# Attention in a macaron block on one core: long matrix products split over neighbouring periods, and two PSUM banks given fixed roles

## The chip, the core and the metric

The kernel runs on one core of a Trainium2 chip. The core has five engines with queues of their own: PE (TensorE, matrix products; PEld is its loading of weights), DVE (VectorE), ACT (ScalarE), POOL (GpSimd) and SP (SyncE, here the issuer of most DMAs). Each queue is worked off in its order; engines meet only through semaphores. Matrix products write to PSUM, which has eight banks of 128 partitions by 512 float32; only DVE and ACT read it here. The metric is the time of one execution in device microseconds, median over several runs; lower is better.

## The reference

The input `x` is 8 sequences of 512 tokens of 512 float32. Three steps follow each other, each on the layer-normalised `x`, and each adds to it:

```
x = x + 0.5 * ffn(layernorm(x))
x = x + attention(layernorm(x))
x = x + 0.5 * ffn(layernorm(x))
```

`ffn` is a router in which each of 16 experts chooses its 256 tokens, all with the same expert matrix: softmax of the logits, a search for the 256th largest value of each expert, and a weighted sum of one product. `attention` is differential: 16 heads of width 32 with 4 key/value heads, and every head has two score maps,

```
q, k = rope(x @ Wq), rope(x @ Wk);  v = x @ Wv
scores = softmax(causal(q_a k_a) / sqrt(D))        # a = 0, 1
diff   = softmax(causal(scores[0] - lam * scores[1]))
att    = rmsnorm(diff @ v) * rms_w * (1 - 0.8 + 0.6)
out    = att @ Wo
```

Everything is float32.

## The kernel before

The order of every engine's queue is written out by hand. `attention` walks over 176 **blocks**: for each of 8 sequences (a batch) and each of two groups of heads (`gp`, a **phase**) eleven blocks, made of the four tiles `i` of 128 queries (tile 0 is one block, tile 1 two, tiles 2 and 3 four each). The loop over `k` is a software pipeline; one turn of it is a **period**. In period `k` five blocks are in work:

- block `k + 1`: its scores on PE (`scores_next`, into banks 0 to 3);
- block `k`: `energies` on DVE (scores plus mask, and their extreme `nb`, from PSUM to `e`), `exps` on ACT (exp, with sums to `z`);
- block `k - 1`: on POOL `mask`, `factors` (after a reciprocal on DVE) and `weigh`; on DVE `difference` (`t`, `nm`);
- block `k - 2`: `exps2` on ACT, the second softmax's exp;
- block `k - 3`: `turn_pe`, transposes on PE into banks 4 and 5, and `turn_copy`, one half on DVE, one on ACT;
- block `k - 4`, if it ends a tile: `values_pe` on PE, `values_out` (`aT`) on DVE.

Beside the blocks goes work that is put into named **slots** of periods: `at(o, slot, fn)` puts it `o` periods behind the start of its phase, and `fill(k, slot)` issues it. These are, in each batch:

- `norm_steps`: layer norm of the next batch (`stats` on DVE, `apply` to `h` on POOL, `turn` to `htp` on PE, `put` to `hT` on ACT);
- `rope_steps`: ten projections, each a **long product** of four matmuls of 128x512 in one bank (L635), two readings of it on DVE (L654, L656), two DMAs that swap neighbouring partitions (L663), an add on POOL (L665);
- `value_steps`: sixteen matmuls of 128x128 for `v` (L610), read by ACT (L618);
- `finish_steps`, four times: squares on ACT, `sums` (`f_ss`, L694 and L700) on PE, `root` on ACT (L707), `turn` (`f_f`, L715) on PE, `norm` on DVE (L723), the output product `f_o` (a long product, L731) and the residual on DVE (L737).

All of these and the value products share banks 6 and 7 (`MISC`), which `misc` gives out in turn. A long product stands in slots "long" and "long 2" of one period, halves `pe(0)` and `pe(1)`, and is read in slot "mid" of the next, behind that period's energies. `PLACES` says for each of the 22 periods of a batch where the scores of the next block stand: ahead of "long" (0), between "long" and "long 2" (1), or behind both (2). Short products stand in slot "short", ahead of all that.

The last phase (`ph == 2 * B - 1`) and the periods behind it also hold the start of the second router (`early_steps`, `drain`), with MISC banks too.

Of the kernel before, what the change touches and what calls it, by code (L numbers as in the profile page):

```python
# [41 lines left out]
def macaron_kernel(  # L42
# [113 lines left out]
    LAST = ((0, 1, 1, 2, 3), (3, 4, 4, 5, 6))  # L156
# [386 lines left out]
    def attention(f0, f1, home, first_end, projections_end, drain):  # L543
        QSCALE = -1.0 / float(D) ** 0.5

        def misc(name):
            return bank(MISC, name)


        def norm_steps(at, b, st):  # L550
# [20 lines left out]
            def apply(i):  # L571
                where, tag = home["h"]
                hs[i] = where.tile([P, E], F32, name=f"h{b}_{i}", tag=tag, bufs=2)
                return nc.gpsimd.tensor_scalar(
                    hs[i], x_sb[b][:, i, :], rstd[:, i : i + 1], nmr[:, i : i + 1],
                    ALU.mult, ALU.add,
                )

            def turn(i):
                ps[i] = misc(f"htp{b}_{i}")  # L580
# [13 lines left out]
            for i in range(TPB):  # L594
                at((0, 0, 3, 3)[i], "dve", lambda i=i: stats(i))
                at((6, 6, 8, 9)[i], "pool", lambda i=i: apply(i))
                at((7, 8, 9, 10)[i], "short", lambda i=i: turn(i))
                at((7, 8, 9, 10)[i], "act mid", lambda i=i: put(i))
# [3 lines left out]
        def value_steps(at, o, b, st):  # L602
            t = {}

            def pe(h):
                if h == 0:
                    t["ps"] = misc(f"vps{b}")
# [12 lines left out]
            at(o, "long", lambda: pe(0))  # L620
            at(o, "long 2", lambda: pe(1))
            at(o + 1, "act first", act)

        def rope_steps(at, o, b, gp, n, st):
# [6 lines left out]
            def pe(h):  # L631
                if h == 0:
                    t["ps"] = misc(f"{name}_ps")
# [32 lines left out]

            at(o, "long", lambda: pe(0))
            at(o, "long 2", lambda: pe(1))
            at(o + 1, "mid", dve)
            at(o + 2, "pool", pool)  # L670

        def finish_steps(at, os, b, i, st):
# [16 lines left out]
            def sums():  # L689


                t["ss"] = misc(f"{name}_ss")
# [17 lines left out]
            def turn():  # L710

                t["f"] = misc(f"{name}_f")
# [14 lines left out]
            def pe(h):  # L727
                if h == 0:
                    t["o"] = misc(f"{name}_o")
# [172 lines left out]
        def values_pe(u):  # L902
# [3 lines left out]
            av = misc(f"av{u['id']}")  # L906
# [78 lines left out]

        def plan(ph):

            b, gp = divmod(ph, 2)
            at = placer(starts[ph])
            if gp == 0:  # L990
# [47 lines left out]
        norm_steps(pre, 0, sts[0])  # L1038
        for n in range(R + 1):
            rope_steps(pre, 12 + n, 0, 0, n, sts[0])  # L1040
# [15 lines left out]
        value_steps(placer(-2), 0, 0, sts[0])  # L1056
        for k in (-2, -1):
            for slot in order:
                fill(k, slot)

# [7 lines left out]
        for k in range(K + 13):  # L1068
            u = blocks[k] if k < K else None
            u1, uE, u2, u3 = (blocks[k - d] if 0 <= k - d < K else None for d in (1, 2, 3, 4))  # L1070
            if k in starts:
                ph = starts.index(k)
                if ph == 2 * B - 1:
# [269 lines left out]
```

## Time and profile before

| | us |
|---|---|
| median of 3 runs | 1421.61 (1421.21 to 1423.42) |
| span of the profiled execution, first to last instruction | 1420.2 |
| attention's phases, from the first scores to the last phase | 204 to 1173 |
| one batch (22 periods) in it | 129.7 |
| PE, DVE, ACT, POOL busy in the span | 1328.5, 1154.9, 1047.0, 685.4 |

The profile gives the profiled execution's own time as its span alone. It is divided by engine and by line of the kernel; a group's row gives busy time, mean duration, and the idle time of the engine ahead of it with what ended it. Matmuls are pipelined and their ends are modelled: a matmul that waits inside its row counts as busy, and durations that start before the row ahead ends overlap. Distances from start to start are therefore the better measure of what a row costs. A row of PE with x8 for four float32 matmuls is right: each is recorded as two passes. "Waits" give waiting engine and tile, releaser, sum in us, times and longest; the chain is the work that ended last, in order of time; the clock is TensorE's granted clock as a share of the full one.

### The profile page before, as it was taken

How to read it: one execution, taken by the hardware profiler on the slowest of the kernel's cores; microseconds unless marked ns; L12 is line 12 of the kernel's file. 1: busy time of each engine (PE TensorE's matmuls, PEld its weight loads, DVE VectorE, ACT ScalarE, POOL GpSimd, SP SyncE). 2: the span in 40 equal slices, each digit the busy share in tenths (PEclk: the TensorE clock that was granted, in tenths of full speed). 3: DMA queues.
4: the chain of work that ended last, by engine and by line, in shares of the span. 5: the costliest groups of instructions: out<-in, count | busy, mean ns of one | idle time of the engine just before them, and what ended most of it. 6: DMA issues, size and time to landing. Idle time of an engine off the chain costs nothing.

```text
span 1420.2 us, 30675 instructions
## 1 busy us (share of the span) xinstructions
PE 1328.5 (94%) x9774; PEld 738.4 (52%) x9774; DVE 1154.9 (81%) x4405; ACT 1047.0 (74%) x3644; POOL 685.4 (48%) x1314
## 2 busy tenths in 40 slices
PE   6999899899999999999999999999999997998998
PEld 4544444455555555555555555555455555555443
DVE  6554769899989988998999899889989989654566
ACT  3411128999899898989898998989899989844110
POOL 5433626554555455454545555554545555443230
PEclk9999988999999999999999999999999997999999
DMA  9300011000000101000000001010000001000006
GB/s 344 91 1 0 0 38 38 9 31 24 16 24 17 39 1 38 9 31 9 32 24 16 28 13 39 2 38 16 24 13 27 28 13 40 1 5 1 1 1 236
DMA packets 27554, 48.19 MB, mean 34 GB/s; under 512 B 4720, under 2 KB 6016, under 8 KB 27392
## 3 DMA queue, kind: packets, MB, share of 16 engines
q1 hardware_dynamic: 25152, 42.03, 8.3%
q10 hardware_dynamic: 2208, 4.19, 0.8%
q8 instruction: 77, 1.26, 0.4%
q14 instruction: 85, 0.70, 0.2%
q0 software_dynamic: 32, 0.01, 0.0%
HBM read 16.86 MB, written 8.39 MB: 18 GB/s over the span
## 4 chain that ended last, share of the span: by engine, by line
PE 60%; ACT 13%; DVE 10%; issue 2%; POOL 0%; ACTq 0%; DVEq 0%
PE r_ps L635 18%; PE sc L761 8%; PE f_o L731 8%; ACT e L790 7%; PE tp L882 6%; PE yps L381 6%; PE av L913 4%; DVE e L777 4%; DVE t L848 3%; ACT t L862 2%; PE vps L610 2%; PE kps L403 2%; PE f_f L715 1%; ACT eT L900 1%; PE tp L325 1%
## 5 line engine op out<-in xcount | busy, mean ns | idle before, releaser
L790 ACT ACTIVATE e<-e,nb 128x192 f32<-128x192 f32 (+7 forms) x1024 | 535.5, 532 | 6.5 <-DVE nb L777 4.3
L777 DVE CUSTOM_DVE_ANT_0 e<-sc,mpos 128x192 f32<-128x192 f32 (+7 forms) x1024 | 400.8, 453 | 23.7 <-PE sc L761 16.5
L814 POOL TENSOR_SCALAR e<-e,z 128x512 f32<-128x512 f32 (+7 forms) x512 | 295.9, 590 | 16.7
L862 ACT ACTIVATE t<-t,nm 128x512 f32<-128x512 f32 (+7 forms) x512 | 270.0, 534 | 42.2 <-DVE nm L848 42.0
L761 PE MATMUL sc<-r,r 32*128 32x64 f32 (+7 forms) x2048 | 245.3, 456 | 10.8 <-DVE nb L777 4.9
L848 DVE CUSTOM_DVE_ANT_0 t<-e,z 128x512 f32<-128x512 f32 (+7 forms) x512 | 240.6, 518 | 5.1 <-POOL e L814 4.2
L635 PE MATMUL r_ps<-hT,wq_sb 128*128 128x512 f32 x512 | 235.6, 601 | 0.1
L381 PE MATMUL yps<-we,y 128*128 128x512 f32 x456 | 216.5, 612 | 1.0 <-ACT y L388 0.7
L882 PEld LDWEIGHTS tp<-ident,t 128*128 128x128 f32 x1280 | 146.5, 144 | 135.6 <-ACT eT L900 43.3
L882 PE MATMUL tp<-ident,t 128*128 128x128 f32 x1280 | 188.6, 283 | 28.1 <-ACT eT L900 26.6
L790 ACT ACTIVATION_READ_ACCUMULATOR e<-e,nb 128x1 f32 x1024 | 202.1, 197 | 0.0
L665 POOL TENSOR_TENSOR r<-r,r_sw 128x512 f32<-128x512 f32 x80 | 103.0, 1296 | 175.8 <-DVE z L799 84.2
L761 PEld LDWEIGHTS sc<-r,r 32*128 32x128 f32 x2048 | 117.4, 188 | 90.7 <-DVE nb L777 44.6
L391 POOL TENSOR_TENSOR y<-y,eb 128x512 f32<-128x512 f32 x57 | 73.1, 1283 | 164.4 <-ACT y L388 134.3
L635 PEld LDWEIGHTS r_ps<-hT,wq_sb 128*128 128x128 f32 x512 | 93.0, 190 | 113.9 <-issue 99.6
L388 ACT COPY y<-yps 128x512 f32<-128x512 f32 x57 | 33.4, 586 | 155.6 <-PE yps L381 155.6
L828 POOL TENSOR_SCALAR_AFFINE_SELECT e<-e 128x128 f32<-128x128 f32 x256 | 79.2, 316 | 99.4 <-ACT e L790 99.4
L898 DVE COPY eT<-tp 128x512 f32<-128x512 f32 (+1 forms) x176 | 112.0, 636 | 16.6 <-PE tp L882 16.6
L381 PEld LDWEIGHTS yps<-we,y 128*128 128x128 f32 x456 | 81.3, 192 | 78.4 <-issue 73.6
L731 PE MATMUL f_o<-wo_sb,f_an 128*128 128x512 f32 x256 | 118.6, 605 | 0.0
L804 POOL TENSOR_TENSOR z<-z,over 128x4 f32<-128x4 f32 (+1 forms) x192 | 38.0, 201 | 142.6 <-DVE z L799 142.5
L862 ACT ACTIVATION_READ_ACCUMULATOR t<-t,nm 128x1 f32 x512 | 100.4, 196 | 0.0
(123 smaller groups left out, 1668.6 us busy)
## 6 DMA issues: line engine op xcount, KB each, us to landing
r_sw<-r_by SPq DMA_DIRECT2D x160, 128.0 KB, 2.0
x<-in_x_dram SPq DMA_DIRECT2D x6, 1024.0 KB, 13.2
out_dram<-x SPq DMA_DIRECT2D x6, 512.0 KB, 3.2
out_dram<-x ACTq DMA_DIRECT2D x6, 512.0 KB, 3.2
x<-in_x_dram SPq DMA_DIRECT2D x8, 256.0 KB, 8.2
we<-in_expert_w_dram SPq DMA_DIRECT2D x2, 1024.0 KB, 7.7
wq_sb<-in_wq_dram SPq DMA_DIRECT2D x1, 2048.0 KB, 13.9
wo_sb<-in_wo_dram SPq DMA_DIRECT2D x8, 128.0 KB, 2.8
```

The lines of the kernel that those rows point to most:

```text
L381: nc.tensor.matmul(held["yps"], buf[b][:, i, c * P : (c + 1) * P], held["we"][:, c, :], start=(c == 0), stop=(c == EC - 1),)
L635: nc.tensor.matmul(t["ps"], w[:, c, c0 : c0 + P], st["hT"][:, c, :], start=(c == 0), stop=(c == EC - 1),)
L665: return nc.gpsimd.tensor_add(t["out"], t["out"], t["sw"])
L731: nc.tensor.matmul(t["o"], t["an"][:, c, :], wo_sb[:, c // 2, c % 2, :], start=(c == 0), stop=(c == 3),)
L761: nc.tensor.matmul(u["sc"][j][:, part.cols], q[j * D : (j + 1) * D, q0 : q0 + P], kq["k"][j * D : (j + 1) * D, : part.n], start=True, stop ...
L777: nc.vector.tensor_tensor_reduce(out=u["e"][:, j, part.cols], in0=u["sc"][j][:, part.cols], in1=mpos[:, S - part.n :], scale=1.0, scalar=3 ...
L790: nc.scalar.activation(e, e, AF.Exp, bias=u["nb"][:, c : c + 1], scale=-1.0, accum_out=u["z"][:, 0, c : c + 1],)
L814: nc.gpsimd.tensor_scalar(e, e, u["z"][:, 1, c : c + 1], u["z"][:, 0, c - nr : c - nr + 1], ALU.mult, ALU.mult,)
L848: u["diff"] = nc.vector.tensor_tensor_reduce(out=u["t"][:, par, r * w : r * w + part.n], in0=u["e"][:, 2 * par, s], in1=u["e"][:, 2 * par ...
L862: nc.scalar.activation(t, t, AF.Exp, bias=u["nm"][:, par, r : r + 1], scale=-1.0, accum_out=z2[:, col : col + 1],)
L882: nc.tensor.transpose(u["tp"][par][:, o : o + P], u["t"][:, par, (r * (i + 1) + c) * P : (r * (i + 1) + c + 1) * P], ident,)
L898: nc.vector.tensor_copy(o, s)
```

## The change

- `product` places a long product in one of three ways. "two": half in slot "long" of period `o` (bank 6), half in "long" of `o + 1`, read in `o + 2` in the new slot "first" (or in ACT's last slot for `v`). "after": both halves in "long 2" of one period, behind the scores (bank 7), read "first" in the next. "one": as it was.
- Slot "first" stands ahead of the reciprocals and the energies of the period's blocks. Six of ten projections of a batch are placed as "two", four as "after"; the values and the output products as "two".
- Bank 7 takes the value products, `htp`, `f_ss`, `f_f` and the "after" products; bank 6 takes the "two" products.
- Short products move from "short" to the new slot "sums", at the end of PE's period; their readers on ACT to its last slot, the norm on DVE to "first" of the next period.
- `values_out` moves ahead of `turn_copy`. `PLACES` holds no longer but in the last phase: the scores stand behind slot "long".
- New tables of places (`ROPES`, `FINISH`); output tile 2 of a phase pair is begun one period earlier; `v` of the next batch moves to the end of phase 0.
- `h` gets a buffer of its own in the pool `proj`; it shared one with the squares.
- The first projections and the last phase ("whole") keep the old way.

```diff
-    LAST = ((0, 1, 1, 2, 3), (3, 4, 4, 5, 6))
+    LAST = ((0, 1, 2, 3), (3, 4, 5, 6))
...
-        def misc(name):
-            return bank(MISC, name)
-
-
-        def norm_steps(at, b, st):
+        WHOLE = 2 * B - 1
+        now = dict(whole=True)
+
+        def misc(name, n=None):
+            return bank(MISC if now["whole"] or n is None else (n,), name)
+
+        def product(at, how, o, pe, slot, read):
+
+            if how == "one":
+                at(o, "long", lambda: pe(0, None))
+                at(o, "long 2", lambda: pe(1, None))
+                at(o + 1, slot, read)
+                return o + 1
+            if how == "after":
+                at(o, "long 2", lambda: pe(0, 7))
+                at(o, "long 2", lambda: pe(1, 7))
+                at(o + 1, "first", read)
+                return o + 1
+            at(o, "long", lambda: pe(0, 6))
+            at(o + 1, "long", lambda: pe(1, 6))
+            at(o + 2 if slot == "mid" else o + 1, "first" if slot == "mid" else "act", read)
+            return o + 2
+
+
+        def norm_steps(at, whole, b, st):
...
-                where, tag = home["h"]
-                hs[i] = where.tile([P, E], F32, name=f"h{b}_{i}", tag=tag, bufs=2)
+                hs[i] = home["h"].tile([P, E], F32, name=f"h{b}_{i}", tag="h", bufs=2)
...
-                ps[i] = misc(f"htp{b}_{i}")
+                ps[i] = misc(f"htp{b}_{i}", None if whole else 7)
...
-                at((7, 8, 9, 10)[i], "short", lambda i=i: turn(i))
-                at((7, 8, 9, 10)[i], "act mid", lambda i=i: put(i))
+                at(7 + i, "short" if whole else "sums", lambda i=i: turn(i))
+                at(7 + i, "act mid" if whole else "act", lambda i=i: put(i))
...
-            at(o, "long", lambda: pe(0))
-            at(o, "long 2", lambda: pe(1))
-            at(o + 1, "act first", act)
-
-        def rope_steps(at, o, b, gp, n, st):
+            product(at, how, o, pe, "act first", act)
+
+        def rope_steps(at, how, o, b, gp, n, st):
...
-            at(o, "long", lambda: pe(0))
-            at(o, "long 2", lambda: pe(1))
-            at(o + 1, "mid", dve)
-            at(o + 2, "pool", pool)
-
-        def finish_steps(at, os, b, i, st):
+            done = product(at, how, o, pe, "mid", dve)
+            at(done + (how == "one"), "pool", pool)
+
+        def finish_steps(at, whole, os, b, i, st):
...
-                t["ss"] = misc(f"{name}_ss")
+                t["ss"] = misc(f"{name}_ss", 7)
...
-                t["f"] = misc(f"{name}_f")
+                t["f"] = misc(f"{name}_f", 7)
...
-            o0, o1, o2, o3, o4 = os
+            o0, o1, o2, o3 = os
             at(o0, "act", square)
-            at(o1, "short", sums)
-            at(o1, "act mid", root)
-            at(o3, "short", turn)
-            at(o3, "dve", norm)
-            at(o4, "long", lambda: pe(0))
-            at(o4, "long 2", lambda: pe(1))
-            at(o4 + 1, "mid", residual)
+            at(o1, "short" if whole else "sums", sums)
+            at(o1, "act mid" if whole else "act", root)
+            at(o2, "short" if whole else "sums", turn)
+            at(o2 if whole else o2 + 1, "dve" if whole else "first", norm)
+            product(at, "one" if whole else "two", o3, pe, "mid", residual)
...
-            av = misc(f"av{u['id']}")
+            av = misc(f"av{u['id']}", 7)
...
+        ROPES = (
+            (("after", 0), ("two", 0), ("after", 2), ("two", 2), ("two", 4)),
+            (("after", 0), ("after", 2), ("two", 1), ("two", 3), ("two", 5)),
+        )
+        FINISH = ((4, 5, 6, 7), (6, 7, 8, 9), (-1, 1, 3, 6), (3, 4, 5, 8))
+        WHOLE_FINISH = ((4, 5, 7, 9), (6, 7, 9, 10), *LAST)
...
-                    for n, o in enumerate((0, 0, 1, 2, 3)):
-                        rope_steps(at, o, b, 1, n, sts[b])
+                    for n, (how, o) in enumerate(ROPES[0]):
+                        rope_steps(at, how, o, b, 1, n, sts[b])
                     if b + 1 < B:
                         sts[b + 1] = new_batch()
-                        norm_steps(at, b + 1, sts[b + 1])
+                        norm_steps(at, False, b + 1, sts[b + 1])
+                        value_steps(at, "two", 10, b + 1, sts[b + 1])
                 if b > 0:
-                    finish_steps(at, (0, 1, 2, 4, 5) if b < B else LAST[0], b - 1, 2, sts[b - 1])
-                    finish_steps(at, (3, 5, 5, 7, 8) if b < B else LAST[1], b - 1, 3, sts[b - 1])
+                    if b == B:
+                        finish(2, b - 1)
+                    finish(3, b - 1)
             else:
                 if b + 1 < B:
-                    for n, o in enumerate((0, 1, 1, 2, 4)):
-                        rope_steps(at, o, b + 1, 0, n, sts[b + 1])
-                    value_steps(at, 3, b + 1, sts[b + 1])
-                finish_steps(at, (4, 5, 5, 7, 9), b, 0, sts[b])
-                finish_steps(at, (6, 7, 7, 9, 10), b, 1, sts[b])
+                    for n, (how, o) in enumerate(ROPES[1]):
+                        rope_steps(at, how, o, b + 1, 0, n, sts[b + 1])
+                finish(0)
+                finish(1)
                 if b == B - 1:
                     for n, os in enumerate(EARLY):
                         early_steps(at, n, *os)
+                else:
+                    finish(2, b, ph + 1, starts[ph + 1] - starts[ph])
...
             fill(k, "short")
+            fill(k, "first")
             if u1 is not None:
                 mask(u1, 0)
                 factors(u1)
...
-            place = PLACES[k % len(PLACES)]
+            place = PLACES[k % len(PLACES)] if now["whole"] else 1
...
             fill(k, "act mid")
             fill(k, "mid")
+            out_early = u3 is not None and u3["last"] and not now["whole"]
+            if out_early:
+                values_out(u3)
             if u2 is not None:
                 turn_copy(u2, 0)
...
-            if u3 is not None and u3["last"]:
+            fill(k, "sums")
+            if u3 is not None and u3["last"] and not out_early:
                 values_out(u3)
...
-        home.update(aT=opened["out"], sq=opened["out"], h=(opened["out"], "sq"))
+        home.update(aT=opened["out"], sq=opened["out"])
```

More of the change, by code (lines that the diff above doesn't have):

```diff
@@ L596, in norm_steps, with value_steps, pe @@
                 at((6, 6, 8, 9)[i], "pool", lambda i=i: apply(i))
-                at((7, 8, 9, 10)[i], "short", lambda i=i: turn(i))
-                at((7, 8, 9, 10)[i], "act mid", lambda i=i: put(i))
+                at(7 + i, "short" if whole else "sums", lambda i=i: turn(i))
+                at(7 + i, "act mid" if whole else "act", lambda i=i: put(i))
             at(3, "act", scale)
             at(4, "mid", shift)
-        def value_steps(at, o, b, st):
+        def value_steps(at, how, o, b, st):
             t = {}
-            def pe(h):
+            def pe(h, n):
                 if h == 0:
-                    t["ps"] = misc(f"vps{b}")
+                    t["ps"] = misc(f"vps{b}", n)
                 for i in (2 * h, 2 * h + 1):
@@ L629, in rope_steps, with pe @@
             t = {}
-            def pe(h):
+            def pe(h, m):
                 if h == 0:
-                    t["ps"] = misc(f"{name}_ps")
+                    t["ps"] = misc(f"{name}_ps", m)
                 for c in (2 * h, 2 * h + 1):
@@ L725, in norm, with pe @@
                 )
-            def pe(h):
+            def pe(h, n):
                 if h == 0:
-                    t["o"] = misc(f"{name}_o")
+                    t["o"] = misc(f"{name}_o", n)
                 for c in (2 * h, 2 * h + 1):
@@ L989, in plan, with finish @@
             at = placer(starts[ph])
+            def finish(i, of=b, ph=ph, shift=0):
+                finish_steps(
+                    lambda o, slot, fn: at(o + shift, slot, fn), ph >= WHOLE,
+                    (WHOLE_FINISH if ph >= WHOLE else FINISH)[i], of, i, sts[of],
+                )
             if gp == 0:
                 if b < B:
-                    for n, o in enumerate((0, 0, 1, 2, 3)):
-                        rope_steps(at, o, b, 1, n, sts[b])
+                    for n, (how, o) in enumerate(ROPES[0]):
+                        rope_steps(at, how, o, b, 1, n, sts[b])
                     if b + 1 < B:
                         sts[b + 1] = new_batch()
-                        norm_steps(at, b + 1, sts[b + 1])
+                        norm_steps(at, False, b + 1, sts[b + 1])
+                        value_steps(at, "two", 10, b + 1, sts[b + 1])
                 if b > 0:
-                    finish_steps(at, (0, 1, 2, 4, 5) if b < B else LAST[0], b - 1, 2, sts[b - 1])
-                    finish_steps(at, (3, 5, 5, 7, 8) if b < B else LAST[1], b - 1, 3, sts[b - 1])
+                    if b == B:
+                        finish(2, b - 1)
+                    finish(3, b - 1)
             else:
                 if b + 1 < B:
-                    for n, o in enumerate((0, 1, 1, 2, 4)):
-                        rope_steps(at, o, b + 1, 0, n, sts[b + 1])
-                    value_steps(at, 3, b + 1, sts[b + 1])
-                finish_steps(at, (4, 5, 5, 7, 9), b, 0, sts[b])
-                finish_steps(at, (6, 7, 7, 9, 10), b, 1, sts[b])
+                    for n, (how, o) in enumerate(ROPES[1]):
+                        rope_steps(at, how, o, b + 1, 0, n, sts[b + 1])
+                finish(0)
+                finish(1)
                 if b == B - 1:
@@ L1037, in attention @@
         pre = placer(-20)
-        norm_steps(pre, 0, sts[0])
+        norm_steps(pre, True, 0, sts[0])
         for n in range(R + 1):
-            rope_steps(pre, 12 + n, 0, 0, n, sts[0])
+            rope_steps(pre, "one", 12 + n, 0, 0, n, sts[0])
         updates = [(b, i) for b in range(1, B) for i in range(TPB)]
@@ L1055, in attention @@
         first_end()
-        value_steps(placer(-2), 0, 0, sts[0])
+        value_steps(placer(-2), "one", 0, 0, sts[0])
         for k in (-2, -1):
@@ L1059, in attention @@
                 fill(k, slot)
+        now["whole"] = False
         PLACES = (1, 0, 1, 2, 2, 0, 0, 0, 0, 0, 2, 0, 0, 0, 0, 0, 0, 0, 0, 0, 0, 0)
@@ L1072, in attention @@
                 ph = starts.index(k)
-                if ph == 2 * B - 1:
+                if ph == WHOLE:
+                    now["whole"] = True
                     projections_end()
@@ L1197, in macaron_kernel @@
     home = dict(
-        hT=proj, kq0=proj, by=proj, sw=proj, h=(proj, "sw")
+        hT=proj, kq0=proj, by=proj, sw=proj, h=proj
     )
```

## The prediction

> **What bounds the kernel now.** I read first the busy time by stretch, one stretch for each batch of the attention, then the waits in one batch, then the chain of waits and the timeline there, then the granted clock. A batch takes 22 periods: two phases (head groups 0 and 1) of eleven periods, 0 to 10, one block a period. In the stretch table the columns after the length are PE, PEld, DVE, ACT, POOL (busy us, instructions), clock, DMA share, GB/s:
>
> ```profile
> 490.30:620.10 129.80, 124.60 (x1072) 70.69 (x1070) 117.77 (x477) 119.67 (x434) 67.87 (x147) 0.96 0.06 22
> 620.10:749.85 129.75, 124.16 (x1077) 70.52 (x1073) 117.69 (x477) 119.87 (x435) 68.56 (x147) 0.99 0.06 22
> 749.85:879.60 129.75, 123.40 (x1077) 70.13 (x1074) 117.65 (x478) 119.99 (x435) 68.85 (x147) 0.99 0.06 22
> ```
>
> Batches repeat to 0.1 us, so one can stand for all. PE looks fullest, but a matmul that waits is shown as a long matmul. Eight records of scores at 448 columns take 1.03 us where nothing holds them and 2.10 where the banks come late:
>
> ```profile
> 634.33 1.03 PE L761 MATMUL sc<-r,r 32*128 32x448 f32 x8
> ...
> 642.21 2.10 PE L761 MATMUL sc<-r,r 32*128 32x448 f32 x8
> ...
> 656.15 3.05 PE L761 MATMUL sc<-r,r 32*128 32x192 f32 x16
> 659.13 5.40 PE L635 MATMUL r_ps<-hT,wk_sb 128*128 128x512 f32 x8
> ...
> 682.56 3.84 PE L610 MATMUL vps<-wv_sb,hT 128*128 128x128 f32 x32
> ```
>
> Adding the unhindered rows for a batch (ten projections and four output products of 3.63, values 3.77, short results 8.8, transposes, scores and value products 48.9) gives PE 112.3 us. So ACT, at 119.9 of 129.75, is the fullest engine, and a batch is ACT's work plus ACT's waits of 9.9 us. These nearly all show (total, times, longest):
>
> ```profile
> ACT t L862 <- DVE nm L848: 5.5, 5, 1.8
> ...
> ACT f_r L707 <- PE f_ss L700: 2.5, 2, 1.4
> ...
> ACT rstd L563 <- DVE mv L560: 0.9, 1, 0.9
> ```
>
> Behind them stands PE. The chain runs on PE alone from 664.5 to 693.7 us and again from 709 to 749, through undivided products:
>
> ```profile
> 666.46 1.08 PE sc L761 x16
> 667.53 7.06 PE r_ps L635 x16
> 674.60 0.87 PE tp L882 x8
> 675.47 0.75 PE sc L761 x8
> 676.22 3.63 PE r_ps L635 x8
> ```
>
> Between those runs the chain lies on ACT and DVE. Engines that each have some 10% to spare wait for each other because the load moves from period to period.
>
> **The change: PE.** Instructions and shapes stay. Durations are start-to-start distances: half a projection 1.82 us, scores 0.75 to 1.10, eight transposes 0.87 (six 0.66), value products 0.59 to 1.09, f_ss 0.6, f_f 1.01, htp 0.59. By the old places PE's work in periods 0 to 10 is 9.0, 7.2, 5.3, 6.4, 3.2, 6.0, 2.7, 3.3, 6.7, 2.3, 3.4 in phase 0 and 5.4, 10.3, 5.3, 6.6, 5.8, 2.3, 2.7, 3.4, 2.4, 6.4, 6.4 in phase 1. By the new ones: 7.2, 5.4, 7.1, 5.6, 4.6, 4.6, 4.5, 4.2, 4.9, 4.2, 5.3 and 7.3, 4.8, 7.1, 4.6, 4.0, 4.2, 5.5, 4.2, 5.3, 3.6, 4.6. (Four of ten projections stay whole, in periods 0 and 2.) ACT's exponentials, copies and small steps come to 7.6, 6.1, 7.3, 5.9, 5.6, 3.8, 4.0, 4.6, 4.9, 4.8, 5.2 and 8.1, 5.4, 7.3, 4.4, 5.8, 4.5, 4.9, 4.8, 4.4, 4.3, 5.7 after. PE, which was above ACT by 0.5 to 4.8 us in nine periods of 22, is above it in six, by 0.9 at most. So long PE runs end: phase 1, periods 0 to 4, goes from 33.3 us of PE (plus the slow product, 5.40 - 3.70 = 1.7) to 27.8, below ACT's 31.0; phase 1 period 9 to phase 0 period 3 from 40.7 to 33.4, below ACT's 36.8 and DVE's 37.0. ACT's 2.5 us for f_ss and the larger part of its 5.5 us for nm go with them: nothing to be carried over but the 0.9 of rstd, whose order is kept.
>
> **What comes instead: DVE.** A read of a projection (1.20 us, two passes of 0.60), the norm (0.60) and the residual (0.60) move from behind the energies to the head of DVE's period, ahead of the reciprocal and energies. They stand so in 13 periods of a batch. Queued behind them are reciprocal (0.2) and the first energy (0.41 to 0.61); ACT waits for that energy with exp, after its second exp of 1.1 to 1.4 us. Where DVE closes a period last, ACT so loses reads + 0.2 + energy + 0.1 of handing over - second exp. Following the queues by hand I find it at four places: phase 1 period 3, two reads, the first held by an undivided product that ends PE's period, 1.15; phase 0 period 4, norm and read, 0.8; period 6, read and norm, 1.0; phase 1 period 9, norm and residual, 0.95. In the other nine I take nothing: either ACT is late itself (period 1: 16 exps, 5.8 us, cover the read) or DVE waits there. Bounds: nothing, and 0.9 at all 13 (11.7). That copy and difference now follow the energies sooner could give ACT something; it is within the 5.5 us of nm, already taken off.
>
> **POOL and the swap DMAs.** A projection's add on POOL (1.30 us) waits for DVE's difference and is now in the read's own period; before, it came one later. Its two DMAs on SP's queue (2.0 us to landing) still have reciprocal, energies, copy and difference, at least 3.9 us, to hide in. What is queued behind the add is next period's mask (0.32), factor (0.20) and weigh (0.61 to 0.72 each), for which the next difference on DVE waits. In phase 0 period 6 the add stands with two applies (0.86): 3.0 us of POOL, then 0.32 + 0.20 + 0.72 to the first weighed map, 4.2, against 0.2 + 2.2 + 0.5 = 2.9 us of DVE; the second half follows 0.7 later. That delays DVE 1.5 us, of which ACT feels 1.1. In phase 1 period 3 two adds, 2.6 us, cost 0.8. Bounds: nothing (the work is the same and only later, so no gain), and 2.5 together.
>
> **Bank 7 and the early copy.** The copy of values (0.20 to 0.42) moves ahead of DVE's transposed copy and costs nothing in sum; the short results now end PE's period and wait for it. It comes right behind the energies for which the scores ahead of them wait as well, so I charge 0.1 in each of five periods, 0.5; bounds 0 and 0.4 each (2.0). The next value product waits for the short result's reader: a period's transposes (0.66 to 0.87) lie between, which hides ACT's 0.47. Scores now always follow the half product (1.8 us later than where they came first); they still lie some 1 us ahead of DVE's need, no charge. The input rows' own buffer for h is worth nothing: POOL's applies wait for DVE, not for it.
>
> **The sum.** ACT waits after: 0.9 + 1.15 + 0.8 + 1.0 + 0.95 + 1.1 + 0.8 + 0.5 = 7.2, against 9.9: 2.7 us a batch. Affected is 204 to 1173 us, 969 / 129.7 = 7.5 batches: 20 us. Front, last phase and second router keep their order. The profiled span 1420.2 goes to 1400; it stands 1.4 below the median of the runs, so 1401.
>
> **The clock.** The granted clock is 0.50 in one window of 3.4 us a batch and 1.00 through a stretch with many short waits:
>
> ```profile
> 659.40:662.80 3.40, 3.40 (x5) 1.35 (x5) 1.15 (x6) 3.40 (x20) 0.87 (x4) 0.50 0.01 2
> 789.10:792.50 3.40, 3.40 (x5) 1.32 (x5) 0.93 (x5) 3.40 (x19) 0.83 (x3) 0.50 0.00 0
> ...
> 642.00:656.00 14.00, 13.40 (x113) 7.94 (x111) 13.39 (x50) 14.00 (x41) 6.92 (x16) 1.00 0.00 1
> ```
>
> The window ahead of the dip held about 1.2 us of real matmul work in 3.4; with the new places I find no stretch below 2.0, so I expect the dips gone. [...]
>
> **Rivals.** (1) Slower: the reads at the head of DVE's period. It lies between reciprocal and energies of every period named. For it: DVE is at 117.7 of 129.75, hardly less full than ACT, so it often closes last. Against: ACT is ahead by up to 5 us in period 0. If all 13 pay 0.9, ACT waits 11.7 + 0.9 + 1.9 + 0.5 = 15.0 a batch, 5.1 more than now: 38 us, 1460. It decides from 7.4 of the 13 on, where 6.6 us of such waits eat up the gain. (2) The queues slip past each other better than by hand, since exp may start on the first map while the rest is late: waits of 3 us are left, 6.9 x 7.5 = 52, 1370. For it: PE's periods are now near equal. Against: DVE's sum with new waits stays close behind ACT's. (3) No change: the dips recur 129.7 us apart, 38 times their 3.41. A gate that takes hold once a batch may keep the batch at that length although work would end earlier; then 1421. Against: it needs a thin window, which I don't find. That the products aren't split can't be: PE's queue has the halves on both sides of the scores.
>
> **How the numbers follow.** My forecast has 0.45, rival 1 0.30, rival 2 0.17, rival 3 0.08. Changes within 0.2% can hardly be told from none in this kernel. That gives faster 0.62, same 0.08, slower 0.30. The forecast alone reaches from 1383 (a third less of waits, 4.8, hence 38 us off) to 1414 (waits of 8.9, 7.5 us off). The range leaves out a tenth at each end: 1370, rival 2, to 1440, half of rival 1's loss.
>
> **What would show it.** Right: batches of about 127 us; ACT's busy time there unchanged at 119.9; no run of PE over 15 us in the chain; waits of ACT's e for DVE's nb, new; clock 1.00 between 300 and 1100 us; DVE's t waiting for POOL's e. Wrong: the wait of e for nb above 7 us a batch, or PE's transposes waiting for ACT's eT more than 2.5 us a batch, which would mean that the end-of-period short results hold PE.

## The result, and the profile after

The changed kernel takes **1428.60 us** (1428.24 to 1429.02) against 1421.64 us for the kernel before on the same chip: a ratio of **1.0046** (95% interval 1.0032 to 1.0060). It is 0.5% slower. I had forecast 1401 us and a gain; the time lies inside the range, the sign on the wrong side. The profiled execution spans 1426.6 us, 6.4 more than before.

The page's head, for the changed kernel: busy time by engine, the granted clock by slices, and the chain's shares.

```profile
span 1426.6 us, 30662 instructions
...
PE 1315.6 (92%) x9774; PEld 709.6 (50%) x9774; DVE 1144.5 (80%) x4405; ACT 1045.4 (73%) x3644; POOL 698.4 (49%) x1314
...
PEclk9999999999999999999999999999999997999999
...
PE 46%; DVE 27%; ACT 15%; POOL 6%; issue 5%; DMA 1%; SPq 0%; POOLq 0%; DVEq 0%; ACTq 0%
```

The last of these lines for the kernel before:

```profile
PE 60%; ACT 13%; DVE 10%; issue 2%; POOL 0%; ACTq 0%; DVEq 0%
```

PE's share of the chain was 60% and is 46%; DVE's went from 10% to 27%, and POOL, the least busy of the four, from 0 to 6%. What was meant to happen on PE did happen for the most part. The stretch table shows what came of it (columns as in the prediction: length, PE, PEld, DVE, ACT, POOL busy, clock, DMA share, GB/s):

```profile
472.00:602.00 130.00, 121.55 (x1073) 66.33 (x1073) 116.31 (x478) 119.91 (x435) 70.62 (x146) 1.00 0.06 22
602.00:732.00 130.00, 121.76 (x1074) 66.32 (x1074) 116.30 (x478) 120.15 (x437) 70.83 (x146) 1.00 0.06 22
732.00:862.00 130.00, 121.44 (x1073) 66.27 (x1072) 116.27 (x478) 119.74 (x435) 70.60 (x146) 1.00 0.06 22
```

In these stretches the clock stays at 1.00 and the dips of every batch are gone; in the six full batches a single one is left, at 0.50 from 437.1 to 440.5 us. ACT's work is the same, and yet a batch takes 130.05 us (from one product of k to the next batch's, 666.58 to 796.63) where it took 129.75. The waits of one batch, 602 to 732 us:

```profile
ACT e L803 <- DVE nb L790: 7.2, 9, 1.4
...
DVE t L861 <- POOL e L827: 2.9, 5, 1.0
...
PE tp L895 <- ACT eT L913: 1.4, 3, 0.6
...
ACT rstd L583 <- DVE mv L580: 0.8, 1, 0.8
...
ACT f_r L722 <- PE f_ss L715: 0.7, 3, 0.3
```

ACT's wait for `nm`, 5.5 us before, has left the list, and that for `f_ss` is down from 2.5 to 0.7. In their place stand 7.2 us for `nb`, the new wait that I had named, and behind it one that matters more than its size: DVE's difference waits 2.9 us for POOL's weigh. In the kernel before (620.1 to 749.85 us) this wait was small:

```profile
DVE t L848 <- POOL e L814: 0.4, 1, 0.4
```

The rest of the 6.4 us lies at the start. The first scores of a phase (rows of 32x64) come at 206.60, 262.87 and 326.81 us before, and at 206.33, 269.96 and 333.65 after: the first phase is 7.4 us longer, the second 0.3 shorter. The six full batches that follow add 1.7 us, 0.7 of it in the first, where the dip at 437 us lies; the first phase of the last batch gives 1.8 back.

### The profile page after: what moved, and what is told of

Same layout as the page of the kernel before. It is cut to its first block, busy times and chain, and to the rows that moved or that the text cites. A ratio compares the mean times of both kernels' runs of the same rounds, so it can differ in the third digit from the quotient of the medians.

```text
span 1426.6 us, 30662 instructions
## 1 busy us (share of the span) xinstructions
PE 1315.6 (92%) x9774; PEld 709.6 (50%) x9774; DVE 1144.5 (80%) x4405; ACT 1045.4 (73%) x3644; POOL 698.4 (49%) x1314
## 4 chain that ended last, share of the span: by engine, by line
PE 46%; DVE 27%; ACT 15%; POOL 6%; issue 5%; DMA 1%; SPq 0%; POOLq 0%; DVEq 0%; ACTq 0%
PE yps L381 14%; PE r_ps L652 11%; ACT e L803 9%; DVE e L790 8%; PE sc L774 5%; DVE t L861 5%; PE f_o L746 4%; ACT t L875 3%; DVE r_by L673 3%; POOL e L827 3%; DVE eT L911 2%; POOL r L682 2%; PE tp L895 2%; PE kps L403 2%; PE tp L325 2%
## 5 line engine op out<-in xcount | busy, mean ns | idle before, releaser
L827 POOL TENSOR_SCALAR e<-e,z 128x512 f32<-128x512 f32 (+7 forms) x512 | 300.4, 600 | 16.7
L652 PE MATMUL r_ps<-hT,wq_sb 128*128 128x512 f32 x512 | 249.8, 618 | 27.3 <-DVE r_by L673 26.3
L861 DVE CUSTOM_DVE_ANT_0 t<-e,z 128x512 f32<-128x512 f32 (+7 forms) x512 | 248.1, 528 | 21.4 <-POOL e L827 20.5
L774 PE MATMUL sc<-r,r 32*128 32x64 f32 (+7 forms) x2048 | 220.7, 451 | 7.4 <-DVE nb L790 3.7
L803 ACT ACTIVATION_READ_ACCUMULATOR e<-e,nb 128x1 f32 x1024 | 193.7, 189 | 0.0
L774 PEld LDWEIGHTS sc<-r,r 32*128 32x128 f32 x2048 | 103.6, 186 | 143.0 <-DVE nb L790 92.8
L652 PEld LDWEIGHTS r_ps<-hT,wq_sb 128*128 128x128 f32 x512 | 89.7, 191 | 129.0 <-issue 87.2
L841 POOL TENSOR_SCALAR_AFFINE_SELECT e<-e 128x128 f32<-128x128 f32 x256 | 87.5, 350 | 103.6 <-ACT e L803 102.9
L746 PE MATMUL f_o<-wo_sb,f_an 128*128 128x512 f32 x256 | 124.7, 611 | 2.0 <-DVE x L752 2.0
L671 DVE SCALAR_TENSOR_TENSOR r<-r_ps,cst 128x512 f32<-128x512 f32 x80 | 55.0, 688 | 76.8 <-PE r_ps L652 76.8
```

Source lines behind the costliest of these rows:

```text
L652: nc.tensor.matmul(t["ps"], w[:, c, c0 : c0 + P], st["hT"][:, c, :], start=(c == 0), stop=(c == EC - 1),)
L746: nc.tensor.matmul(t["o"], t["an"][:, c, :], wo_sb[:, c // 2, c % 2, :], start=(c == 0), stop=(c == 3),)
L774: nc.tensor.matmul(u["sc"][j][:, part.cols], q[j * D : (j + 1) * D, q0 : q0 + P], kq["k"][j * D : (j + 1) * D, : part.n], start=True, stop ...
L803: nc.scalar.activation(e, e, AF.Exp, bias=u["nb"][:, c : c + 1], scale=-1.0, accum_out=u["z"][:, 0, c : c + 1],)
L827: nc.gpsimd.tensor_scalar(e, e, u["z"][:, 1, c : c + 1], u["z"][:, 0, c - nr : c - nr + 1], ALU.mult, ALU.mult,)
L861: u["diff"] = nc.vector.tensor_tensor_reduce(out=u["t"][:, par, r * w : r * w + part.n], in0=u["e"][:, 2 * par, s], in1=u["e"][:, 2 * par ...
```

## The experiments

Every kernel does the whole work. Times are medians; ratios are to the kernel before, with 95% intervals.

### The add on POOL one period later

```diff
-            at(done + (how == "one"), "pool", pool)
+            at(done + (how != "after"), "pool", pool)
```

> The changed kernel, with POOL's add of each divided projection one period later (as far behind its read as it was before the change). Theory B, the add in the read's own period holds up mask, factor and weigh of the next period and by them the difference on DVE (DVE's t waits 2.9 us a batch for POOL's e in the changed kernel, behind 4 periods): these waits go, and 1.9 us of ACT's 7.2 a batch with them, 14 us in 7.5 batches, about 1414. Rival, DVE is the bound there and the wait only moves: ACT's wait of e for nb stays at 6 to 7 us a batch, and the time within 3 us of 1428.6.

Measured: **1405.1 us** (1403.85 to 1406.15), ratio 0.9880 (0.9866 to 0.9895). This one line is worth 23.5 us. The six "two" products of a batch have their adds behind one more block's weigh; nothing else moves. (The four "after" products keep theirs in the read's own period.) In the changed kernel POOL's timeline in phase 0, period 6, reads (start, length, line, what; in brackets the idle time ahead and what ended it):

```profile
642.54 1.30 POOL L682 TENSOR_TENSOR r<-r,r_sw 128x512 f32<-128x512 f32 x1 [1.98 <-DVE z L812]
643.83 1.52 POOL L593 TENSOR_SCALAR h<-x,rstd,nmr 128x512 f32<-128x512 f32 x2
645.30 0.29 POOL L841 TENSOR_SCALAR_AFFINE_SELECT e<-e 128x128 f32<-128x128 f32 x1
645.56 0.20 POOL L817 TENSOR_TENSOR z<-z,over 128x4 f32<-128x4 f32 x1
645.86 1.68 POOL L827 TENSOR_SCALAR e<-e,z 128x384 f32<-128x384 f32 x2
```

The add and two applies, 2.8 us, start when DVE's difference is done (an order written into slot "pool"), and the weigh starts 3.3 us behind the add's start. DVE's timeline there shows what that costs, and ACT's row what is handed on: the energy that follows comes late.

```profile
646.56 0.62 DVE L861 CUSTOM_DVE_ANT_0 t<-e,z 128x384 f32<-128x384 f32 x1 [1.01 <-POOL e L827]
...
647.58 0.62 DVE L861 CUSTOM_DVE_ANT_0 t<-e,z 128x384 f32<-128x384 f32 x1 [0.40 <-POOL e L827]
```

```profile
649.58 0.72 ACT L803 ACTIVATE e<-e,nb 128x512 f32<-128x512 f32 x1 [0.62 <-DVE nb L790]
```

In phase 1, period 3, the chain itself goes through the add, the mask, the factor and the weigh to DVE's difference:

```profile
692.49 1.29 POOL r L682
693.78 0.25 POOL e L841
694.03 0.17 POOL z L817
...
694.30 1.52 POOL e L827 x2
...
695.85 0.04 DVE t L861
```

With the add later, POOL's timeline at the same place has the applies alone, and the add in the next period:

```profile
632.85 1.52 POOL L593 TENSOR_SCALAR h<-x,rstd,nmr 128x512 f32<-128x512 f32 x2 [1.99 <-DVE z L812]
...
634.89 1.31 POOL L827 TENSOR_SCALAR e<-e,z 128x384 f32<-128x384 f32 x2
637.24 1.32 POOL L682 TENSOR_TENSOR r<-r,r_sw 128x512 f32<-128x512 f32 x1 [1.04 <-DVE nm L861]
```

DVE waits for POOL nowhere in that kernel's batch, POOL's share of its chain is 1%, and the batch is 126.86 us (592.28 to 719.14). Its stretch and ACT's wait:

```profile
592.00:719.00 127.00, 120.68 (x1078) 65.77 (x1073) 115.99 (x478) 119.74 (x435) 69.87 (x146) 1.00 0.06 22
```

```profile
ACT e L803 <- DVE nb L790: 4.8, 7, 1.5
```

The batch is 3.2 us shorter, and 7.5 batches make 24: the whole gain. (Measured between first scores of phases, batches without a dip take 126.84 to 127.14 us instead of 129.75 to 130.04, some 3.0 less.) DVE's 2.9 us for POOL are gone, and 2.4 of ACT's 7.2 for `nb`, which were the same delay handed on: they go at the energies behind DVE's waits, in phase 0 periods 6 (1.44 to 0.74) and 8 (0.62 to nothing) and in phase 1 period 5 (1.00 to nothing).

### One add alone, and the same edit in the kernel before

```diff
+            at(done + (how == "one" or (how, o) == ("two", 4)), "pool", pool)
```

> The changed kernel, with one add alone a period later: the one that stands in phase 0, period 6 with the two applies of h on POOL (3.0 us of POOL in a row). All six divided projections' adds a period later gave 1405.1, 23.5 us less than the changed kernel. By the prediction's prices (1.1 us for this place, 0.8 for the two adds of phase 1 period 3) this add has over half: 1.1/1.9 of 23.5, 13.6 us, so 1415. Rival, each of the six adds costs alike because it always stands ahead of the next mask and weigh: a sixth, 4 us, 1424.6.

Measured: 1425.68 us (1422.48 to 1429.49), ratio 1.0022 (1.0010 to 1.0035): 2.9 us of 23.5. Moving this add takes half of DVE's wait for POOL away (2.9 to 1.5 us a batch). Four of the six full batches in the trace take 129.0 us, 0.7 to 1.0 less than in the changed kernel; the other two take 130.5 and 130.7 (592.58 to 723.27). The granted clock's mean over the span is 0.975 here and 0.980 in the changed kernel. So the lump with the two applies is worth up to a third of the 3.0 us a batch, less than the 1.1 of 1.9 that its price made it, and in two batches of six that is lost again. The whole gain comes only when all six are out of the way.

```diff
-            at(o + 2, "pool", pool)
+            at(o + 1, "pool", pool)
```

> The kernel before, with every projection's add on POOL one period earlier, in the period in which DVE reads the product; nothing else is changed. Theory B, an add right behind its read stands ahead of the next mask and weigh while the swap's DMAs have just been issued: slower than before by 1 to 3 us a batch, 8 to 23 us, 1430 to 1445. Rival, only the new order has so little slack on DVE: the kernel before, in which PE closes most periods, hides it, and stays within 3 us of 1421.6.

In the kernel before this gives 1438.69 us (1436.07 to 1442.4), ratio 1.0115 (1.0095 to 1.0134): 16 us lost, and POOL in its chain (3%, from 0). There the read is late in the period, and the swap's DMAs stand in the way too. The waits in 130 us of that kernel (592 to 722):

```profile
POOL r L665 <- DMA r_sw<-r_by: 9.6, 2, 6.7
...
ACT t L862 <- DVE nm L848: 7.2, 8, 1.8
...
DVE t L848 <- POOL e L814: 3.4, 5, 2.1
```

DVE's wait for POOL, 0.4 us a batch in the kernel before, is 3.4.

So the early add costs in both kernels, by partly different waits.

### Adds and applies that needn't wait for the difference

```diff
-            fill(k, "pool", after=u1 and u1["diff"])
+            fill(k, "pool")
```

> The changed kernel, but what stands in slot pool (the projections' adds and the norm's applies) no longer has to wait for DVE's difference of its period; its place in POOL's queue stays. In the changed kernel POOL is idle for 1.98 us ahead of the add at 642.54, then add, applies, mask, factor and weigh follow, and DVE waits 1.01 and 0.40 us for that weigh. Theory: the price of the early add is this order, wait for the difference, then 1.3 us ahead of the weigh. Then it goes when the add may start in that idle time: no wait of DVE's t for POOL's e (2.9 us a batch now), batches near 127 us, 1405, as with the add one period later. Rival: it is the 1.3 us themselves, or POOL's work beside DVE's, that cost. Then DVE's rows get longer where the add lies beside them, or the waits stay, and the time stays at 1425 or above.

Measured: 1464.13 us (1459.71 to 1467.08), ratio 1.0279 (1.0261 to 1.0298), 36 us worse than the changed kernel. DVE's waits for POOL are gone, as the theory had it, but the rival's first sign, longer rows on DVE, is there too: its rows of 256 columns for the difference take 880 ns on average where they took 479, and DVE is busy 124 to 125 us a batch where it was 116. So this run can't say what the waiting alone costs; a larger cost took its place.

> The version with the add one period later and the new reading order (1398.6 us), and the same wait for the difference taken out. There DVE never waits for POOL, so theory expects no gain from an earlier start: 1398 to 1400. Rival, work of POOL beside DVE's energies costs DVE time: seven batches of ten adds and four applies, at 0.1 us each 1.4 us a batch, 1409.

On top of the best version (below): 1442.14 us (1441.12 to 1448.09), ratio 1.0144 (1.0122 to 1.0166), 43.5 us worse than with the wait. Where POOL's add runs beside DVE's difference, a row of the difference gets longer. DVE's and POOL's timelines in this kernel:

```profile
632.82 0.45 DVE L861 CUSTOM_DVE_ANT_0 t<-e,z 128x256 f32<-128x256 f32 x1
...
633.20 1.56 DVE L861 CUSTOM_DVE_ANT_0 t<-e,z 128x256 f32<-128x256 f32 x1
...
634.69 0.50 DVE L861 CUSTOM_DVE_ANT_0 t<-e,z 128x256 f32<-128x256 f32 x1
```

```profile
633.17 1.30 POOL L682 TENSOR_TENSOR r<-r,r_sw 128x512 f32<-128x512 f32 x1 [0.48 <-DMA r_sw<-r_by]
```

A row of 0.45 us takes 1.56 beside an add of 1.30. Over a batch DVE's busy time is 121.02 us against 116.17, 4.85 more, and the batch is 5.0 longer (130.91 against 125.91). Three of the six full batches are longer still, 131.5 to 132.6 us; the granted clock's mean over the span is 0.974 here and 0.980 with the wait in place. The 0.1 us that the rival takes for work beside the energies was a guess, and the means don't show it: energies of 128x384 take 547 ns here and 548 with the wait. The written-out order is there for a reason: it keeps add and difference apart. It also means that an add can only choose which weigh it stands in front of.

### Which read comes first

```diff
+            at(done + (how != "after"), "pool", pool)
...
-            (("after", 0), ("after", 2), ("two", 1), ("two", 3), ("two", 5)),
+            (("after", 0), ("two", 1), ("after", 2), ("two", 3), ("two", 5)),
```

> The kernel with all adds later (1405.1), and in phase 1 the second and third projection exchanged, so that in period 3 DVE reads the divided product, which is long finished, while it waits for the undivided one (a wait of 2.16 us in the trace), and not behind it. ACT's wait of e for nb is 1.46 us there. Theory C: 1.2 us a batch less (one read of two passes), 9 us in 7.5 batches, 1396. Rival, period 3 is closed by something else, DVE's share of later work being the same: the 1.2 us come back as a wait in periods 4 to 6, within 2 us of 1405.

Measured: **1398.62 us** (1397.72 to 1399.47), ratio **0.9831** (0.9816 to 0.9846), 6.5 us less than with the late add alone. In phase 1, period 3, two products are read at the head of DVE's period; the one read first was the one that PE had only just finished. With the late add alone DVE's and ACT's rows there are:

```profile
673.85 0.69 DVE L671 SCALAR_TENSOR_TENSOR r<-r_ps,cst 128x512 f32<-128x512 f32 x1 [2.16 <-PE r_ps L652]
...
676.90 0.56 ACT L803 ACTIVATE e<-e,nb 128x320 f32<-128x320 f32 x1 [1.46 <-DVE nb L790]
```

With the finished product read first, its 1.2 us fit into the wait (DVE's row, then ACT's):

```profile
671.54 0.69 DVE L671 SCALAR_TENSOR_TENSOR r<-r_ps,cst 128x512 f32<-128x512 f32 x1 [0.96 <-PE r_ps L652]
...
673.39 0.56 ACT L803 ACTIVATE e<-e,nb 128x320 f32<-128x320 f32 x1 [0.24 <-DVE nb L790]
```

DVE saves 1.2 us and ACT 1.2; the batch goes from 126.86 to 125.91 us, 0.95. This version beats both kernels: 24 us under the one before, 30 under the changed one.

### The reads at the head of DVE's period

```diff
-                at(o + 1, "first", read)
+                at(o + 1, "mid", read)
...
-            at(o + 2 if slot == "mid" else o + 1, "first" if slot == "mid" else "act", read)
+            at(o + 2 if slot == "mid" else o + 1, "mid" if slot == "mid" else "act", read)
```

> The changed kernel, with the reads of long products and the residuals behind the energies again (the norm stays at the head). Theory C, the reads at the head of DVE's period are what ACT's e waits for (7.2 us a batch): that wait falls below 3 us, and the time by up to 4 us a batch, 30 us, to 1399, if PE's next half finds bank 6 free in time. Rival D, bank 6 is then free only behind the energies, PE's half waits for the read in every period with two products following each other (10 a batch, 1 to 2 us each) and the scores behind it with it: slower than 1428.6 by 10 us or more, with PE's r_ps waiting for DVE's r_by above 8 us a batch instead of 2.9.

Measured: 1611.03 us (1610.45 to 1614.3), ratio 1.1335 (1.1313 to 1.1356). Behind the energies, as before the change, the reads leave a bank too late: PE's next half waits for `r_by` (7.8 us a batch), POOL for the swap's DMAs (18.6), ACT for `f_ss` (16.7):

```profile
POOL r L682 <- DMA r_sw<-r_by: 18.6, 5, 4.5
...
ACT f_r L722 <- PE f_ss L715: 16.7, 4, 4.8
...
PE r_ps L652 <- DVE r_by L673: 7.8, 3, 2.8
```

So the new places of the halves can't be had without the early reads here, where one bank serves all divided products.

```diff
-            fill(k, "first")
...
             if u is not None:
                 energies(u, (0,))
+            fill(k, "first")
```

> The changed kernel, with the reads between the first energy of the period and the other three, and behind the reciprocal, so that ACT's first exp and POOL's weigh needn't wait for them. Theory C: the first exp starts 0.6 to 1.8 us earlier, but the second map then waits for the read; about half of the 7.2 us goes, 3.6 x 7.5 = 27, to 1402. Rival, DVE closes these periods last whatever stands at their head, and so the wait moves to the second map (e for nb stays at 6 us or more): within 4 us of 1428.6. By rival D bank 6 comes free 0.8 us later in each such period, which would cost up to 0.8 x 10 x 7.5 = 60 at most.

Measured: 1435.98 us (1431.79 to 1440.43), ratio 1.0098 (1.0066 to 1.0131). One energy ahead of the reads does lower ACT's wait for `nb`, from 7.2 to 5.0 us, but ACT's wait for `f_ss` rises from 0.7 to 4.5 and DVE's reciprocal waits 8.3 us for ACT. My rival 1, the reads as the main loss, isn't cured by moving them.

### Undivided products

```diff
-            at(o + 1, "long", lambda: pe(1, 6))
+            at(o if slot == "mid" else o + 1, "long", lambda: pe(1, 6))
```

> The kernel with all adds later (1405.1), and the products that were divided undivided: both halves in slot long of the first of the two periods, ahead of the scores, read where they were read (the values, whose second half needs later input, stay divided). Places, banks and reads as in the changed kernel. Theory E, the even share of PE's work is what the gain comes from: PE's periods are again up to 6 us apart, ACT waits for PE by 3 us a batch or more, 1405 + 23 = 1428 or above. Rival, what helps is the order around them (reads ahead, banks apart), and a product that is ready a period before its read costs nothing: within 4 us of 1405.

Measured, with the late add: 1474.4 us (1473.32 to 1479.7), ratio 1.0361 (1.0344 to 1.0378), 69 us more than with the halves apart; a batch is 137.3 us (619.36 to 756.65). With the late add but without the division the new order is 52 us slower than the kernel before; with both it is 18 us faster.

### Three smaller terms, on the version at 1398.6 us

Norm's scale and shift one period later, against ACT's 0.8 us for `rstd`:

```diff
-            at(3, "act", scale)
-            at(4, "mid", shift)
+            at(3 if whole else 4, "act", scale)
+            at(4 if whole else 5, "mid", shift)
```

> The kernel at 1398.6, with the layer norm's root on ACT and the shift on DVE one period later (periods 4 and 5 of phase 0 instead of 3 and 4). ACT waits 0.82 us a batch for the statistics there. If a wait of ACT on this place is worth its length: 0.8 x 7.5 = 6 us less, 1392.5. If DVE closes these periods, the wait comes back in the next exp: within 1.5 us of 1398.6.

Measured: 1399.35 us (1398.36 to 1401.74), no gain: the wait disappears from the list and ACT's wait for `nb` grows from 3.9 to 4.4.

The scores ahead of the half product:

```diff
-            place = PLACES[k % len(PLACES)] if now["whole"] else 1
+            place = PLACES[k % len(PLACES)] if now["whole"] else 0
```

> The kernel at 1398.6, with the next block's scores ahead of the half product instead of behind it. By the prediction's step (scores behind the half cost nothing, as they still lie 1 us ahead of DVE's need) nothing is to be gained: within 3 us, or slower, since the half then waits behind scores that wait for the energies (PE's wait for nb is 10 us a batch for its weights' loading in the trace with all adds later). Rival, the scores come late for DVE in periods with an undivided product (DVE's e waits for sc): up to 4 us less.

Measured: 1586.55 us (1583.87 to 1587.46), ratio 1.1154 (1.1133 to 1.1176). DVE's reads then wait 19.2 us a batch for their products, and ACT 11.8 for `f_ss`. Nothing is to be had by putting the scores ahead; behind the half, DVE waits for them 0.3 us a batch.

The copy of values behind DVE's transposed copy:

```diff
+                turn_copy(u2, 1)
+            if out_early:
+                values_out(u3)
```

> The kernel at 1398.6, with the copy of the values product behind DVE's transposed copy again (both still ahead of the short results). By the prediction's step the early copy saves the short results in five periods a batch one copy of 0.5 to 0.6 us of waiting: up to 0.5 x 5 x 7.5 = 19 us slower if PE's end of period decides, 0 if ACT or DVE does. I expect 3 to 8 us slower, about 1404.

Measured: 1400.12 us (1398.69 to 1400.85), 1.5 more, hardly beyond the spread.

### The lost time in the first phase

Phase 0 of the first batch in its old places and with the old norm:

```diff
+        OLD_ROPES = tuple(("one", o) for o in (0, 0, 1, 2, 3))
...
-                    for n, (how, o) in enumerate(ROPES[0]):
+                    for n, (how, o) in enumerate(OLD_ROPES if ph == 0 else ROPES[0]):
...
-                        norm_steps(at, False, b + 1, sts[b + 1])
+                        norm_steps(at, ph == 0, b + 1, sts[b + 1])
```

> The changed kernel, with the first phase alone (blocks 0 to 10, when no older block is in work) in the old places. Comparing the traces of before and changed, the first phase is 7.4 us longer in the changed one (206.3 to 270.0 us instead of 206.6 to 262.9), which is more than the whole difference of 6.4 us in the spans. Theory A, the new order itself makes the first phase long, because the undivided k product stands ahead of DVE's reciprocal and nothing else is there to be done: 7 us less than the changed kernel, about 1421.5. Rival, the first phase is long because of the clock (four windows at 0.50 between 222 and 260 us, three in before) or for a start-up reason that the places don't touch: within 2 us of 1428.6.

Measured: 1428.2 us (1425.48 to 1428.34), ratio 1.0039 (1.0023 to 1.0054), no gain. The first phase is short again (206.28 to 265.13), but the second takes 70.1 us where it took 63.7: the time moves to the crossing into the new order.

The same on the version at 1398.6 us, with the bank at the crossing mended:

```diff
+                    t["ps"] = misc(f"vps{b}") if n is None else bank((n,), f"vps{b}")
```

> The kernel with all adds later and the reads of phase 1 period 3 exchanged (1398.6), with the first phase in the old places, and the first values product held in bank 6 (in the earlier trial of the old first phase the k product behind it waited 3.5 us for the copy of v and then ran 3.1 us long at half clock). Theory A, the new places make the first phase 7 us longer, and the earlier trial lost this at that one crossing: 6 to 7 us less, 1392. Rival, it is the lead that the new places have to build up once, wherever they begin: within 2 us of 1398.6.

Measured: 1398.02 us (1395.87 to 1399.79), ratio 0.9831 (0.9811 to 0.9851), again no gain.

The new order with the first four reads of phase 0 behind the energies; in the changed kernel two of them, at the head of DVE's period, hold it longest of all:

```profile
214.87 0.69 DVE L671 SCALAR_TENSOR_TENSOR r<-r_ps,cst 128x512 f32<-128x512 f32 x1 [3.02 <-PE r_ps L652]
...
230.14 0.69 DVE L671 SCALAR_TENSOR_TENSOR r<-r_ps,cst 128x512 f32<-128x512 f32 x1 [3.98 <-PE r_ps L652]
```

```diff
-                at(o + 1, "first", read)
+                at(o + 1, "mid" if now["lead"] and o < 3 else "first", read)
...
-            at(o + 2 if slot == "mid" else o + 1, "first" if slot == "mid" else "act", read)
+            at(o + 2 if slot == "mid" else o + 1, "act" if slot != "mid" else "mid" if now["lead"] and o < 3 else "first", read)
```

> The version at 1398.6 us, but in the first phase the first four projections are read behind the energies instead of ahead of them. In its first phase DVE waits 3.02 us (at 216.2) and 3.83 us (at 231.4) for a product at the head of a period, and ACT behind it 6.4 us. Theory: these two waits are the one-time loss of about 7 us at the start of the attention, so the time is some 5 to 6.5 us less, 1392 to 1394. Rival, the loss belongs to the crossing to the steady order and only moves, as it did where the whole old first phase was put back: 1398 to 1399.

Measured: 1403.26 us (1400.51 to 1403.68), ratio 0.9858 (0.9843 to 0.9873), 4.6 worse. The two long waits go from DVE, but PE then waits 9.1 us for the reads (4.5 without this edit), 5.6 at once, and the first phase is 67.0 us instead of 62.9.

> Both at once: the first phase's four reads behind the energies, and no wait for the difference ahead of the adds. If both are independent, the sum of the two single effects, to 1 us; by the theory 1392 to 1395. If the adds' freedom costs only in the steady batches, it shows here as it does without the new first phase.

Measured: 1445.53 us (1441.06 to 1446.36), ratio 1.0153 (1.0135 to 1.0170). The two losses, 4.6 and 43.5, add to within 1.3 us.

So the first phase's 7 us are no loose end that one edit takes off; three ways to it gave nothing or a loss. What sets them stays open.

## Why the prediction was wrong

**The step that failed: "POOL and the swap DMAs".** I priced the earlier add at 1.1 and 0.8 us a batch in two places, the adds elsewhere at nothing, and bounded the whole at 2.5. It costs 3.0 to 3.2 a batch, 23.5 us in all: above the bound and more than the gain forecast. Behind the add of phase 0 period 6, DVE waits 1.4 us (I had 1.5) and ACT 0.6 (I had 1.1). Behind those of phase 1 period 3, the two wait 1.1 and 1.0. But the add of phase 0 period 4, put at nothing, costs 0.4 and 0.7. The rest of the 3.0 is spread: 0.1 of `nb`, 0.2 of `f_ss`, and 0.3 in ACT's own rows. I called the work "the same and only later", although DVE, by my own table hardly less full than ACT, passes a delay on to the next energies; and I compared it with POOL's work, not with the place that the add would leave. Why a period later is free I can only argue: there the next period opens with a read, a norm or a residual on DVE (0.6 to 1.8 us), so the weigh is ready when DVE gets to it. The five waits in the changed kernel fit this: all lie in periods that open with none of these (phase 0 periods 5 and 7, phase 1 period 4).

**A second step: "What comes instead: DVE", and the sum.** Without the POOL term my waits are 5.3 us a batch, 125.2 in length; with the late add the kernel shows 7.1 and 126.86. These missing 1.7 us, 13 over 7.5 batches, have two halves. About 0.9 are waits for `nb`. At the four places named I forecast 3.9 us, and with the late add they sum to 3.3 (phase 0 period 4 0.57, period 6 0.74, phase 1 period 3 1.46, period 9 0.50); that they come to 3.95 in the changed kernel is luck, as 0.7 of it is POOL's. "In the other nine I take nothing" was wrong: with the late add phase 0 period 3 costs 0.95 and phase 1 period 7 0.44. The other half is waits that the sum left out: the three it started from come to 8.9 of its 9.9, the last 1.0 was dropped without a reason, and ACT now waits 0.4 us for the norm's transposes and 0.3 for POOL's `z`.

**A term that wasn't in the sum.** From 1401 to 1428.6 the miss is 27.6 us: 9.4 from the add (3.15 instead of 1.9 a batch), 13 from the second step, and some 5 from the start, where the first phase is 7.4 us longer and 2.1 come back in the second phase and in the last batch. That the new order has to be built up once is a reading that no run shows.

**Right.** PE's runs in the chain of that batch are shorter, at most 19.5 us (697.67 to 717.13) where they were 29 and 40, though my sign was none over 15. The waits for `nm` are gone and most of that for `f_ss`; ACT's work is unchanged; the batch of "about 127 us" is there once the add is out of the way. The clock is 1.00 between 300 and 1100 us but for the dip at 437.1 us. That thin work of PE brings a dip was my estimate, and the runs don't show it: PE is busy for 1.50 of the 3.41 us ahead of this dip (433.73 to 437.14), where I had found no stretch below 2.0, but also for 1.40 each of 694.90 to 698.31, 824.90 to 828.31 and 954.70 to 958.11, and there the clock stays at 1.00. Bank 7 doesn't hold PE's transposes (1.4 us, under my mark of 2.5). The early copy costs nothing.

**The rivals.** Rival 1 had the sign, by another mechanism: `nb` stands at 7.2, just above my mark of 7 for it, and 2.4 of that is POOL's. Rival 3, a time locked to the clock's windows, has no support: the dips went and the batch found a length of 130.05, 126.86 or 125.91, none of them a whole number of the 3.41 us that a dip lasts (659.40 to 662.81 in the kernel before): 38.1, 37.2 and 36.9. With products in banks 6 and 7 all along, the granted clock stays at 1.00 from 440.6 to 1184 us.

## What to carry to other kernels

When a change brings a result forward on one engine, follow each consumer to its own queue and ask what it now stands in front of: here an engine that is busy half the time (POOL, 49%) decided the sign. Removing a wait on the fullest engine needn't be worth its length (0.8 us gave nothing, 1.2 gave 0.95), so price the place that the work leaves as well as the one it takes. Of several products read at the head of a period, read the finished one first.

## What the runs showed of the hardware

A row of DVE's difference gets longer beside POOL's add: with the adds free on the best version, a 128x256 row took 1.56 us instead of 0.45 while a 1.30 us add ran, and the eight such rows of a batch average 747 ns against 478. DVE's energies and reads keep their means (128x384 energies 547 ns with the adds free, 548 with them held; reads 688 and 690 ns). Why the difference gets longer, no run shows.

Small changes of order can cost much: reads behind the energies or scores ahead of the half cost 13% against the versions that they were made from, with no instruction added. In both of them the granted clock's mean over the span falls (0.927 and 0.947 against 0.980); how much of the 13% is the clock's isn't separated.
